# Joining two key classes of a softmax by copies and a one-input reduce in place of small two-input operations

## The chip, the cores and the metric

The kernel runs on one core of a Trainium2 chip. The metric is device time in microseconds (us), the median of several executions; lower is better. The engines are TensorE (PE, matrix products; PEld is its loading of weights), VectorE (DVE), ScalarE (ACT), GpSimd (POOL) and SyncE (SP, which issues the DMAs here). Each engine works through its own list of instructions in the order written, and waits at an instruction until what that one needs is there.

## The reference

All data are f32. With x of 4 sequences x 1024 positions x 1024 features, 32 heads of 32 features, it computes

```python
x = x + attention(layernorm(x), wq, wk, wv, wo)      # rotary q and k, causal softmax
x = x + ffn(layernorm(x), route_w, A, Bw)            # each token goes to the best of 8 rank-16 adapters

scores = jnp.einsum('bqhd,bkhd->bhqk', q, k) * scale
scores = jnp.where(causal, scores, finfo.min)
probs  = jax.nn.softmax(scores, axis=-1)
out    = jnp.einsum('bhqk,bkhd->bqhd', probs, v).reshape(b, s, d) @ wo
```

The softmax needs the largest score of each row (query) and the sum of its exponentials. Those are the "maxima" and "totals" of the title.

## The kernel before, in words

**Units.** The attention is done in 32 units (`attend`): 4 sequences x 8 groups of 4 heads. While one unit's softmax runs, PE also has dense work for other units: the projections to q, k and v (`group`, the products `pa_*` and `pb_*` of line 816) and, for finished sequences, the output projection and the adapters (`finish_tile`, `po` of line 1389, `ph`, `pf`).

**A tile of scores.** A unit has 16 tiles t of 64 queries, handled in 11 rounds (`ROUNDS`): the eight long tiles one to a round, the eight short ones in rounds of 2, 2 and 4. The 128 partitions of a tile hold four groups i of 32: two halves of 32 queries, and for each half two *classes of keys*, the even and the odd blocks of 32 keys. So every row of the softmax is split over two neighbouring groups of partitions, i and i ^ 1, and both its maximum and its total have to be joined across them.

**Steps of a round.** PE makes the scores `s` in PSUM (line 1027); there is one such buffer of four banks, and the value products `av` use it too. ACT copies them to SBUF (`pr` or `pr_low`, line 1060). POOL adds the causal mask on the diagonal (line 1066). DVE takes each class's negated maximum (`top`, line 1088) with `tensor_reduce`. DVE joins the classes (`both`, line 934, in `with_other`): four `tensor_tensor` minima, one for each group of 32 partitions, whose two inputs lie in different groups. ACT computes the exponentials with `both` as bias and leaves each class's sum in `den` (line 1121, an ACTIVATE and a READ_ACCUMULATOR for each head). DVE transposes the blocks of 32x32 (line 1145). After the last round of a quad (4 tiles) PE multiplies by the values (`apply_quad`, `av`, line 1190), and ACT takes the result out of PSUM (`at`, line 1230).

**Totals.** After half a unit (a block, 64 in all) `finish_block` joins the two classes of `den` with four DVE additions (`rec_sb`, line 1254), takes reciprocals (1255), transposes them (1257), sends them through DRAM to spread them over partitions (`by`), and POOL multiplies (`at`, line 1285).

**Layer norm.** `moments` (lines 373 to 386) makes mean, variance, the inverse deviation `rstd` and `less`, which is minus mean times `rstd`. `scale_x` (line 437) applies it on DVE for 8 tiles of the first sequence; elsewhere ACT applies `rstd` and `less`.

**What sets the order.** Nothing is issued where it stands in the source. Every step is a `Task` with an engine, a guessed duration, a due position `pos` (lower is sooner) and the tasks and buffers that it needs. `Plan.order` simulates the five engines once, when the kernel is built, and so writes the order of each engine's instructions. The planner gives `both` 0.72 us. Scores are form "S" on PE, values form "V", all else "D". Three constants matter here: `FETCH`, the time that the planner grants for a block of 256 PE instructions to be fetched; `PATIENCE`, a time after its readiness in which a value task is passed over if PE has other work; `SIGNAL`, the delay from one engine to another.

Of the kernel before, what the change touches and what calls it, by code (L numbers as in the profile page):

```python
# [9 lines left out]
F32 = mybir.dt.float32  # L10
AF = mybir.ActivationFunctionType
ALU = mybir.AluOpType
AX = mybir.AxisListType

P = 128
# [4 lines left out]
SQ = 32  # L20
# [8 lines left out]
DENSE = 0.859  # L29


CHANGE, BLOCK, FETCH = 0.2, 256, 4.5

PATIENCE = 1.0


def act_us(n):
    return 0.05 + 0.000836 * n


def dve_us(n):
    return 0.09 + 0.00103 * n
# [33 lines left out]
class Plan:  # L76
# [23 lines left out]
    def order(self):  # L100
# [91 lines left out]
        def finished(t, now):  # L192
            for b in {id(b): b for b in [*t.uses, *t.opens]}.values():
                b.users -= 1
                if not b.users:
                    at(now + (0.5 if b.slots.name[0] != "_" else 0.25), (b,))
            far = SIGNAL.get(t.engine, 0.1)
            for x in t.next:
                near = x.engine == t.engine and x.engine != "SP"
                when = now + (0.0 if near else far)  # L200
                came[x.number] = max(came.get(x.number, 0.0), when)
                x.waits -= 1
                if not x.waits:
                    at(came[x.number], x)
# [54 lines left out]
def tile_preln_attn_then_top1_lora(  # L259
# [104 lines left out]
    def moments(pos, src, name, after):  # L364

        got = {}

        def stats(i):
            if i == 0:
                got["st"] = small.tile(  # L370
                    [P, D // HALF, nc.vector.BN_STATS_DIM], F32, tag="stats", bufs=5, name=f"st_{name}"
                )
            nc.vector.bn_stats(got["st"][:, i, :], src.tile[:, i * HALF : (i + 1) * HALF])

        def gather():
            got["mv"] = small.tile([P, nc.vector.BN_AGGR_DIM], F32, tag="mv", bufs=5, name=f"mv_{name}")
            nc.vector.bn_aggr(got["mv"], got["st"])
            got["ve"] = small.tile([P, 1], F32, tag="ve", bufs=5, name=f"ve_{name}")
            nc.vector.tensor_scalar(got["ve"], got["mv"][:, 1:2], EPS, None, ALU.add)
            got["less"] = got["mv"][:, 1:2]  # L380
            nc.vector.tensor_scalar(got["less"], got["mv"][:, 0:1], -1.0, None, ALU.mult)

        def power():
            got["rstd"] = small.tile([P, 1], F32, tag="rstd", bufs=5, name=f"rstd_{name}")
            nc.gpsimd.tensor_tensor(got["rstd"], got["ve"], half_sb, ALU.pow)
            nc.gpsimd.tensor_tensor(got["less"], got["less"], got["rstd"], ALU.mult)

        t = None
        for i in range(D // HALF):
            t = add("DVE", 0.61, lambda i=i: stats(i), pos, [after[i], t], [src])  # L390
        t = add("DVE", 0.45, gather, pos, [t])
        t = add("POOL", 0.8, power, pos, [t, cleared])
        return got, t
# [29 lines left out]
    def take_x(b, t, pos):  # L423
        src = sbuf(rows if t % 5 > 2 else feeds, [P, D], f"x_{b}_{t}", "x")
        load = add(
            "SP",
            0.4,
            lambda: nc.sync.dma_start(src.tile, x[b, t * P : (t + 1) * P, :]),
            pos,
            opens=[src],  # L430
            size=P * D * 4,
        )
        soon = pos - FIRST
        got, m = moments(soon, src, f"a{b}_{t}", [load, load])

        def scale_x():
            nc.vector.tensor_scalar(
                src.tile, src.tile, got["mv"][:, 0:1], got["rstd"], ALU.subtract, ALU.mult
            )

        m = add("DVE", 0.75, scale_x, soon, [m], [src])
        tb, k = divmod(t, TB)

        both = [A[b, f"A{tb + 1}{half + 1}"] for half in range(2)]

        def keep(half):
            if k == 0:
                return [], [], [both[half]]
            return [turned_x[b, t - 1, half]], [both[half]], []

        def dst(half):
            return both[half].tile[:, :, k * P : (k + 1) * P]

        for half, d in enumerate(turn(dst, src, f"a{b}_{t}", soon, [m], keep)):
            turned_x[b, t, half] = d
# [471 lines left out]
    def width(k):  # L927
        return (QUADS - 1) * pitch(k) + QUADS * (k + 1) * SQ

    def with_other(dst, src, op):  # L930

        for i in range(P // SQ):
            r, o = slice(i * SQ, (i + 1) * SQ), slice((i ^ 1) * SQ, ((i ^ 1) + 1) * SQ)
            nc.vector.tensor_tensor(dst[r], src[r], src[o], op)  # L934

    total_cols = sum((t + 1) for r in ROUNDS[0] for t in r)
    prob_ready, av_done = {}, {}

    def attend(b, g):
        u = b * NG + g  # L940
# [63 lines left out]
        for tiles in rounds:  # L1004
# [74 lines left out]
            for k, t in enumerate(tiles):  # L1079
                step = HG if t < 8 else 2  # L1080
                for h in range(0, HG, step):

                    def top(k=k, t=t, h=h, step=step, got=got, n=n, tiles=tiles):
                        if "top" not in got:
                            got["top"] = small.tile(
                                [P, n, HG], F32, tag=f"top{n}", bufs=3, name=f"top_{u}_{tiles[0]}"
                            )
                        nc.vector.tensor_reduce(  # L1088
                            got["top"][:, k, h : h + step],
                            place(t)[:, h : h + step, :],  # L1090
                            AX.X,
                            ALU.max,
                            negate=True,
                        )

                    reduced.append(
                        add(
                            "DVE",
                            dve_us(step * (t + 1) * SQ),
                            top,  # L1100
                            pos - 20,
                            [masked[t]],
                            [quads[quad]],
                        )
                    )

            def join(got=got, n=n, tiles=tiles):
                got["both"] = small.tile(
                    [P, n, HG], F32, tag=f"both{n}", name=f"both_{u}_{tiles[0]}", bufs=9 if n == 1 else 3
                )  # L1110
                with_other(got["both"], got["top"], ALU.min)

            joined = add("DVE", 0.72, join, pos - 20, reduced)
            for k, t in enumerate(tiles):
                blk = t // 8
                of_t = []
# [55 lines left out]
    def apply_quad(u, quad, pos, where, vt, loads, turned, of_blk):  # L1172
# [33 lines left out]
        for i in range(n):  # L1206
            js = range(i * nj // n, (i + 1) * nj // n)
            last = add(
                "PE",
                0.01 + 0.215 * len(js),  # L1210
                lambda js=js: piece(js),
                pos - 60,
                [*turned, *loads, last],
                [pr, vt, whole],
                [whole] if i == 0 else [],
                form="V",
                ins=32 * len(js),
            )
        blk, second = divmod(quad, 2)
        if blk not in of_blk:  # L1220
            of_blk[blk] = {"done": sbuf(dones, [P, HALF], f"at_{u}_{blk}"), "steps": []}
# [3 lines left out]
        for half in range(2):  # L1225

            def take(half=half):
                dst = done.tile.rearrange("p (q t s k) -> p q s t k", q=2, s=2, k=SQ)
                src = whole.tile[:, half, : QUADS * SQ].rearrange("p (t k) -> p t k", k=SQ)
                nc.scalar.copy(dst[:, second, half], src)  # L1230

            of_blk[blk]["steps"].append(
                add(
                    "ACT",
                    act_us(QUADS * SQ),
                    take,
                    pos - 100,
                    [last],
                    [whole, done],
                    [done] if first_of_block and half == 0 else [],  # L1240
                )
            )

    def finish_block(b, g, blk, pos, exps, dens, of_blk):
        u = b * NG + g
        done, steps = of_blk[blk]["done"], of_blk[blk]["steps"]
        got = {}

        def join_sums():
            of_den = dens[blk].rearrange("p (t c) h -> p c h t", c=2)  # L1250
            rec = rec_sb[:, blk, : HG * TB].rearrange("p (h t) -> p h t", t=TB)
            for i in range(P // SQ):
                r, o = slice(i * SQ, (i + 1) * SQ), slice((i ^ 1) * SQ, ((i ^ 1) + 1) * SQ)
                nc.vector.tensor_tensor(rec[r], of_den[r, i % 2], of_den[o, i % 2], ALU.add)  # L1254
            nc.vector.reciprocal(rec_sb[:, blk, : HG * TB], rec_sb[:, blk, : HG * TB])
            got["turned"] = small.tile([P, SQ], F32, tag="recT", name=f"recT_{u}_{blk}")
            nc.vector.transpose(got["turned"], rec_sb[:, blk])

        t = add("DVE", 1.2, join_sums, pos - 20, [*exps[blk], cleared])
        there = dram.tile(  # L1260
            [HG * TB, P // SQ, SQ], F32, tag=f"recs{u}_{blk}", name=f"recs_{u}_{blk}"
        )
# [392 lines left out]
```

## Time and profile before

| what | us |
|---|---|
| median of 3 runs | 2819.16 (2813.59 to 2820.26) |
| the profiled execution, its own time | 2805.12 |
| its span, from the first to the last instruction | 2802.9 |
| DVE busy in the span | 2216.6 |
| ACT busy in the span | 1862.3 |
| POOL busy in the span | 1007.0 |

The profiled execution is one run beside the three, some 14 us under their median. The profile counts an engine as busy while one of its instructions executes; PE's matmuls are pipelined and their ends are modelled. A row of waits counts the time in which an engine stood idle and names the work that released it. The chain of waits goes back from the last instruction, at every step to what released it or to the instruction before it on the same engine. "issue" is time in which an engine waited for nothing that the profile shows. The mean granted clock of TensorE was 0.976 of full speed.

### The profile page before, as it was taken

The page shows a single profiled execution, that of the slowest core. Times are in us where ns is not written, and L with a number is a line of the kernel's source. Part 1 is how long each engine was busy: PE and PEld are TensorE (multiplying, and loading weights), DVE is VectorE, ACT ScalarE, POOL GpSimd, SP SyncE. Part 2 cuts the span into 40 slices and gives each one's busy share as a digit, 9 for nine tenths or more (in the row PEclk, how much of TensorE's full clock was granted, in tenths as well). Part 3 has the DMA queues.
Part 4 walks back from the last instruction along what each step waited for, and adds up shares of the span by engine and source line. Part 5 has one row for each costly group of instructions (what it writes and reads, how often), then busy time and mean ns, then how long its engine had stood idle before and what let it go on. Part 6 is the DMA issues. An engine that isn't in the chain of part 4 may idle for free.

```text
span 2802.9 us, 100252 instructions
## 1 busy us (share of the span) xinstructions
PE 2606.1 (93%) x41960; PEld 1277.9 (46%) x41960; DVE 2216.6 (79%) x4450; ACT 1862.3 (66%) x5320; POOL 1007.0 (36%) x1227
## 2 busy tenths in 40 slices
PE   7888989899999999999989999999999999989898
PEld 6433444444444444444444444444444444444454
DVE  7786887989788897888898886789788777977632
ACT  2585766778678687777777785667577565865511
POOL 3437464534353423333333442323333232331100
PEclk9989999999999999999999999999999999999999
DMA  5545354854457757655666675665756555565221
GB/s 176 156 132 178 111 170 127 251 154 124 139 166 210 223 168 258 203 169 169 198 191 191 207 222 156 199 237 175 210 152 194 164 159 177 172 210 174 92 88 55
DMA packets 398500, 484.01 MB, mean 173 GB/s; under 512 B 37856, under 2 KB 252128, under 8 KB 395360
## 3 DMA queue, kind: packets, MB, share of 16 engines
q1 hardware_dynamic: 398048, 477.62, 56.0%
q8 instruction: 329, 5.39, 0.8%
q14 instruction: 123, 1.01, 0.1%
HBM read 358.47 MB, written 119.01 MB: 170 GB/s over the span
## 4 chain that ended last, share of the span: by engine, by line
PE 54%; DVE 29%; ACT 5%; issue 4%; POOL 3%; DMA 2%; SPq 0%; POOLq 0%; ACTq 0%; DVEq 0%
PE po L1389 12%; DVE top L1088 9%; PE pa_qk L816 8%; PE av L1190 8%; PE s L1027 7%; DVE both L934 7%; PE pb_qk L816 6%; DVE pr L1145 6%; PE pa_v L816 4%; PE pb_v L816 3%; ACT pr_low L1121 2%; PE ph L1448 2%; PE pf L1523 2%; DVE rec_sb L1254 1%; DVE pr_low L1145 1%
## 5 line engine op out<-in xcount | busy, mean ns | idle before, releaser
L1121 ACT ACTIVATE pr<-pr,both 128x512 f32<-128x512 f32 (+7 forms) x1024 | 635.7, 634 | 71.6 <-DVE both L934 70.6
L1088 DVE TENSOR_REDUCE top<-pr 128x2 f32<-128x768 f32 (+7 forms) x512 | 477.5, 970 | 126.3 <-POOL pr L1066 124.9
L1389 PE MATMUL po<-wo,attn 128*128 128x512 f32 x1024 | 502.5, 615 | 2.2 <-DMA wo<-in_wo 1.5
L1145 DVE STREAM_TRANSPOSE pr<-pr 128x768 f32<-128x768 f32 (+7 forms) x512 | 481.7, 983 | 11.7 <-ACT pr L1121 8.5
L1121 ACT ACTIVATE pr_low<-pr_low,both 128x256 f32<-128x256 f32 (+7 forms) x1024 | 412.6, 416 | 68.6 <-DVE both L934 68.3
L1060 ACT COPY pr<-s 128x2048 f32<-128x2048 f32 (+7 forms) x256 | 381.0, 1488 | 95.5 <-PE s L1027 84.4
L1027 PE MATMUL s<-k,q 32*32 32x256 f32 (+7 forms) x16384 | 389.5, 407 | 50.4 <-ACT pr L1060 23.9
L934 DVE TENSOR_TENSOR both<-top 32x4 f32<-32x4 f32 (+2 forms) x1408 | 370.0, 263 | 29.2
L1066 POOL TENSOR_TENSOR pr<-pr,causal_sb 128x128 f32<-128x128 f32 x256 | 116.8, 456 | 635.7 <-ACT pr L1060 623.7
L1190 PE MATMUL av<-pr,val 64*32 64x128 f32 (+2 forms) x14336 | 241.3, 270 | 82.5 <-issue 50.6
L1027 PEld LDWEIGHTS s<-k,q 32*32 32x32 f32 x16384 | 155.8, 104 | 327.2 <-ACT pr L1060 107.2
L1190 PEld LDWEIGHTS av<-pr,val 64*32 64x32 f32 x14336 | 206.4, 108 | 186.5 <-issue 127.2
L1389 PEld LDWEIGHTS po<-wo,attn 128*128 128x128 f32 x1024 | 183.1, 193 | 209.5 <-issue 194.9
L1230 ACT COPY at<-av 128x128 f32<-128x128 f32 x256 | 54.9, 267 | 272.5 <-PE av L1190 272.5
L729 POOL TENSOR_TENSOR r_qk<-r_qk,cos_sb 128x512 f32<-128x512 f32 x124 | 158.2, 1276 | 215.8 <-DVE swq L720 98.5
L816 PE MATMUL pa_qk<-A,T_qk 128*128 128x512 f32 x440 | 214.4, 607 | 0.0
L1088 DVE TENSOR_REDUCE top<-pr_low 128x4 f32<-128x1024 f32 (+7 forms) x256 | 177.7, 739 | 41.5 <-POOL pr_low L1066 40.9
L1121 ACT ACTIVATION_READ_ACCUMULATOR pr<-pr,both 128x1 f32 x1024 | 209.0, 204 | 0.0
L1145 DVE STREAM_TRANSPOSE pr_low<-pr_low 128x1024 f32<-128x1024 f32 (+7 forms) x256 | 184.3, 753 | 29.6 <-ACT pr_low L1121 27.7
L1121 ACT ACTIVATION_READ_ACCUMULATOR pr_low<-pr_low,both 128x1 f32 x1024 | 205.8, 201 | 0.0
L1060 ACT COPY pr_low<-s 128x1024 f32<-128x1024 f32 (+7 forms) x256 | 147.7, 639 | 80.9 <-PE s L1027 80.8
L1066 POOL TENSOR_TENSOR pr_low<-pr_low,causal_sb 128x128 f32<-128x128 f32 x256 | 112.0, 455 | 231.6 <-ACT pr_low L1060 228.3
(128 smaller groups left out, 3680.7 us busy)
## 6 DMA issues: line engine op xcount, KB each, us to landing
wo<-in_wo SPq DMA_DIRECT2D x352, 256.0 KB, 3.5
val<-vd SPq DMA_DIRECT2D x128, 256.0 KB, 5.6
T_qk<-t_qk SPq DMA_DIRECT2D x96, 256.0 KB, 3.5
x<-in_x SPq DMA_DIRECT2D x32, 512.0 KB, 5.4
q<-qd SPq DMA_DIRECT2D x128, 128.0 KB, 3.6
b_qk<-in_wq SPq DMA_DIRECT2D x64, 256.0 KB, 3.8
k<-kd SPq DMA_DIRECT2D x32, 512.0 KB, 5.2
vd<-vt SPq DMA_DIRECT2D x64, 256.0 KB, 3.2
```

The lines of the kernel that those rows point to most:

```text
L729: lambda: nc.gpsimd.tensor_tensor(raw.tile, raw.tile, cos_sb[:, cols], ALU.mult),
L816: nc.tensor.matmul(at.tile, lhsT=buf.tile[:, c, :], rhs=act.tile[:, c, :], start=first_ and c == 0, stop=c == KC - 1, skip_group_check=not ...
L934: nc.vector.tensor_tensor(dst[r], src[r], src[o], op)
L1027: nc.tensor.matmul(s.tile[i * SQ : (i + 1) * SQ, h, at : at + w].rearrange("p (j k) -> p j k", k=SQ), lhsT=of_q[r, 2 * (t % QUADS) + half] ...
L1060: nc.scalar.copy(place(t), s.tile[:, :, at : at + w])
L1066: nc.gpsimd.tensor_tensor(diagonal, diagonal, causal_sb.unsqueeze(1).to_broadcast([P, HG, SQ]), ALU.add,)
L1088: nc.vector.tensor_reduce(got["top"][:, k, h : h + step], place(t)[:, h : h + step, :], AX.X, ALU.max, negate=True,)
L1121: nc.scalar.activation(pr[:, h, :], pr[:, h, :], AF.Exp, bias=got["both"][:, k, h : h + 1], accum_out=den(blk)[:, t % 8, h : h + 1],)
L1145: nc.vector.transpose(pr, pr)
L1190: nc.tensor.matmul(whole.tile[h * HD : (h + 1) * HD, half, t0 * SQ : QUADS * SQ].rearrange("p (t k) -> p t k", k=SQ), lhsT=vt.tile[r, h, j ...
L1389: nc.tensor.matmul(po.tile, lhsT=at.tile[:, c * P : (c + 1) * P], rhs=w.tile[:, c % KC] if kept else w.tile, start=c == 0, stop=c == NC - 1,)
L1448: nc.tensor.matmul(ph.tile, lhsT=yn.tile[:, c * P : (c + 1) * P], rhs=w.tile[:, c if kept else c - c0, :], start=c == 0, stop=c == NC - 1,)
```

## The change

The maxima are joined in two steps: `top` gets a second column for each head, four ACT copies write the other class's maxima into it (`swap_classes`, a task of its own ahead of the exponentials), and one DVE `tensor_reduce` over the two columns gives the minimum. The totals are treated alike: four ACT copies of `den` into `denx`, four additions, which now run on POOL, and the reciprocal and transpose on DVE as a task of its own. In the planner FETCH goes from 4.5 to 4.8, PATIENCE from 1.0 to 0, and LATE is new: a task of form S or V that waits for another engine's work counts as ready 1.0 us later. Two dependencies are added (a quad's values wait for the values before them in the unit; the copies out of PSUM wait for the block's first). In the layer norm two results overwrite their inputs, and `scale_x` multiplies by `rstd` and adds `less`.

```diff
-CHANGE, BLOCK, FETCH = 0.2, 256, 4.5
-
-PATIENCE = 1.0
+CHANGE, BLOCK, FETCH = 0.2, 256, 4.8
+
+PATIENCE = 0.0
+
+LATE = 1.0
...
-                when = now + (0.0 if near else far)
+                when = now + (0.0 if near else far + LATE * (x.form in "SV"))
...
-            got["ve"] = small.tile([P, 1], F32, tag="ve", bufs=5, name=f"ve_{name}")
-            nc.vector.tensor_scalar(got["ve"], got["mv"][:, 1:2], EPS, None, ALU.add)
-            got["less"] = got["mv"][:, 1:2]
-            nc.vector.tensor_scalar(got["less"], got["mv"][:, 0:1], -1.0, None, ALU.mult)
+            got["ve"], got["less"] = got["mv"][:, 1:2], got["mv"][:, 0:1]
+            nc.vector.tensor_scalar(got["ve"], got["ve"], EPS, None, ALU.add)
+            nc.vector.tensor_scalar(got["less"], got["less"], -1.0, None, ALU.mult)
...
-                src.tile, src.tile, got["mv"][:, 0:1], got["rstd"], ALU.subtract, ALU.mult
+                src.tile, src.tile, got["rstd"], got["less"], ALU.mult, ALU.add
...
-    def with_other(dst, src, op):
+    def swap_classes(dst, src):
         for i in range(P // SQ):
             r, o = slice(i * SQ, (i + 1) * SQ), slice((i ^ 1) * SQ, ((i ^ 1) + 1) * SQ)
-            nc.vector.tensor_tensor(dst[r], src[r], src[o], op)
+            nc.scalar.copy(dst[r], src[o])
...
-                                [P, n, HG], F32, tag=f"top{n}", bufs=3, name=f"top_{u}_{tiles[0]}"
+                                [P, n, HG, 2], F32, tag=f"top{n}", bufs=3, name=f"top_{u}_{tiles[0]}"
...
-                            got["top"][:, k, h : h + step],
+                            got["top"][:, k, h : h + step, 0],
...
+            def swap(got=got):
+                swap_classes(got["top"][:, :, :, 1], got["top"][:, :, :, 0])
+
...
-                with_other(got["both"], got["top"], ALU.min)
-
-            joined = add("DVE", 0.72, join, pos - 20, reduced)
+                nc.vector.tensor_reduce(got["both"], got["top"], AX.X, ALU.min)
+
+            swapped = add("ACT", 4 * act_us(n * HG), swap, pos - 100, reduced)
+            joined = add("DVE", dve_us(2 * n * HG), join, pos - 50, [swapped])
...
-                [*turned, *loads, last],
+                [*turned, *loads, last or values_done.get(u)],
...
-                    [last],
+                    [last, *of_blk[blk]["steps"][:1]],
...
+        def swap():
+            got["den"] = small.tile([P, 2 * QUADS, HG], F32, tag="denx", name=f"denx_{u}_{blk}", bufs=1)
+            swap_classes(got["den"], dens[blk])
+
         def join_sums():
-            of_den = dens[blk].rearrange("p (t c) h -> p c h t", c=2)
             rec = rec_sb[:, blk, : HG * TB].rearrange("p (h t) -> p h t", t=TB)
             for i in range(P // SQ):
-                r, o = slice(i * SQ, (i + 1) * SQ), slice((i ^ 1) * SQ, ((i ^ 1) + 1) * SQ)
-                nc.vector.tensor_tensor(rec[r], of_den[r, i % 2], of_den[o, i % 2], ALU.add)
+                r = slice(i * SQ, (i + 1) * SQ)
+                pair = [d[r].rearrange("p (t c) h -> p c h t", c=2)[:, i % 2] for d in (dens[blk], got["den"])]
+                nc.gpsimd.tensor_tensor(rec[r], *pair, ALU.add)
+
+        def turn_sums():
             nc.vector.reciprocal(rec_sb[:, blk, : HG * TB], rec_sb[:, blk, : HG * TB])
...
-        t = add("DVE", 1.2, join_sums, pos - 20, [*exps[blk], cleared])
+        t = add("ACT", 4 * act_us(2 * QUADS * HG), swap, pos - 20, [*exps[blk]])
+        t = add("POOL", 0.8, join_sums, pos - 20, [t, cleared])
+        t = add("DVE", 0.45, turn_sums, pos - 20, [t])
```

More of the change, by code (lines that the diff above doesn't have):

```diff
@@ L928, in width @@
         return (QUADS - 1) * pitch(k) + QUADS * (k + 1) * SQ
-    def with_other(dst, src, op):
+    def swap_classes(dst, src):
         for i in range(P // SQ):
             r, o = slice(i * SQ, (i + 1) * SQ), slice((i ^ 1) * SQ, ((i ^ 1) + 1) * SQ)
-            nc.vector.tensor_tensor(dst[r], src[r], src[o], op)
+            nc.scalar.copy(dst[r], src[o])
     total_cols = sum((t + 1) for r in ROUNDS[0] for t in r)
-    prob_ready, av_done = {}, {}
+    values_done = {}
     def attend(b, g):
@@ L1218, in apply_quad @@
             )
+        values_done[u] = last
         blk, second = divmod(quad, 2)
```

## The prediction

> **What bounds the kernel now.** I read the page's busy shares first, then its chain of waits, then the list of who waited for whom for TensorE (PE) alone, then groups by shape, then the timeline of a few microseconds in the middle.
>
> Page, first part and fourth part:
>
> ```profile
> PE 2606.1 (93%) x41960; PEld 1277.9 (46%) x41960; DVE 2216.6 (79%) x4450; ACT 1862.3 (66%) x5320; POOL 1007.0 (36%) x1227
> ...
> PE 54%; DVE 29%; ACT 5%; issue 4%; POOL 3%; DMA 2%; SPq 0%; POOLq 0%; ACTq 0%; DVEq 0%
> PE po L1389 12%; DVE top L1088 9%; PE pa_qk L816 8%; PE av L1190 8%; PE s L1027 7%; DVE both L934 7%; PE pb_qk L816 6%; DVE pr L1145 6%; PE pa_v L816 4%; PE pb_v L816 3%; ACT pr_low L1121 2%; PE ph L1448 2%; PE pf L1523 2%; DVE rec_sb L1254 1%; DVE pr_low L1145 1%
> ```
>
> PE is busy 93% of a span of 2802.9 us, so at most about 197 us can go without making PE's own work shorter. Yet the chain runs through VectorE (DVE) for 29%, and through `both`, 1408 instructions on at most 32x16 elements, for 7%, 196 us. So PE is the bound that is never far, and DVE decides when the next attention matmul may start. What PE really stands still for is in its waits (total us, times, longest):
>
> ```profile
> PE av L1190 <- issue: 54.9, 36, 4.4
> PE s L1027 <- ACT pr L1060: 23.9, 18, 3.3
> PE av L1190 <- DVE pr L1145: 17.1, 14, 3.4
> PE s L1027 <- ACT pr_low L1060: 15.8, 10, 3.9
> PE av L1190 <- DVE pr_low L1145: 14.1, 6, 5.4
> ...
> PE s L1027 <- ACT at L1230: 9.3, 7, 2.0
> ...
> PE av L1190 <- ACT pr_low L1121: 7.8, 1, 7.8
> ```
>
> Scores (`s`) wait for ScalarE (ACT) to empty the one PSUM buffer: 23.9 + 15.8 + 9.3 = 49.0 us. Values (`av`) wait for transposes and exponentials: 17.1 + 14.1 + 7.8, and 8.4 in three smaller rows, 47.4 us. Together 96.4 us is what faster maxima can win on PE. Another 54.9 us is "issue": PE waits for nothing that the profile shows. The other 46 us belong to transposes, weights and the end, which the change hardly touches.
>
> Why `both` costs what it does, from the timeline (start, duration, engine, line) and groups (busy us, mean ns, idle before):
>
> ```profile
> 1404.04 1.28 POOL L737 TENSOR_TENSOR swk<-swk,sin_sb 128x512 f32<-128x512 f32 x1
> 1404.33 2.84 DVE L934 TENSOR_TENSOR both<-top 32x8 f32<-32x8 f32 x4
> 1405.69 1.27 POOL L745 TENSOR_TENSOR r_qk<-r_qk,swk 128x512 f32<-128x512 f32 x1
> 1408.04 1.37 ACT L1060 COPY pr_low<-s 128x512 f32<-128x512 f32 x4
> ```
>
> ```profile
> L934 DVE TENSOR_TENSOR both<-top 32x4 f32<-32x4 f32 x1024 | 254.2, 248 | 21.2
> L1121 ACT ACTIVATION_READ_ACCUMULATOR pr<-pr,both 128x1 f32 x1024 | 209.0, 204 | 0.0
> L1060 ACT COPY pr_low<-s 128x512 f32<-128x512 f32 x32 | 18.2, 569 | 7.7 <-PE s L1027 7.7
> L1060 ACT COPY pr_low<-s 128x128 f32<-128x128 f32 x32 | 8.9, 277 | 0.0
> L1475 DVE TENSOR_REDUCE best<-rank 128x1 f32<-128x8 f32 x32 | 5.2, 161 | 1.1
> L386 POOL TENSOR_TENSOR mv_a<-mv_a,rstd_a 128x1 f32<-128x1 f32 x32 | 6.1, 189 | 2.5
> ```
>
> Four tiny minima at 1404.33 take 2.84 us; one of them starts under the POOL instruction that runs from 1404.04 and ends with it, another likewise with that of 1405.69. Counted over the trace: 1016 of the 1408 overlap no POOL instruction and take 156 ns on average; 392 do and take 540 ns. `tensor_reduce` (`top`) shows no such thing: 887 ns without, 900 ns with POOL beside it. A round's four with the gaps between them take 0.707 us at the median, 1.10 us at the mean, over 352 rounds 387 us.
>
> **The change part by part.**
>
> *Maxima.* Removed from DVE: 352 rounds x 1.10 = 387 us. Added to DVE: 352 reduces of 8 to 32 elements, no wait on POOL, by the `best` row 0.161 us: 57 us. Added to ACT: 352 x 4 copies of 4 to 16 elements. None is in the trace. The nearest rows are score copies: (569 - 277) / 384 = 0.76 ns an element, so 4 elements take 277 - 124 x 0.76 = 183 ns; and four copies that would take 569 + 477 + 376 + 277 = 1699 ns (the group's four shapes) stand in 1.37 us, so each hides 0.11 us behind the next. Four tiny ones: 4 x 0.183 - 3 x 0.11 = 0.40 us; 352 x 0.40 = 141 us of ACT. Lower end 0.30 us (the shortest distance from the start of a 512-element copy to the next instruction's is 465 ns, of a 128-element one 145 ns, so 0.83 ns an element and 38 ns each besides, plus one full duration): 106 us. Upper end no overlap at the READ_ACCUMULATOR's 204 ns: 0.82 us, 287 us. I take 0.40.
>
> The Trainium skill ("ScalarE: Activation LUTs", What ACT_TABLE_LOAD costs) speaks against such copies: it gives a small instruction 186 ns and back-to-back ones an overlap of only about 93 ns. By that page, an estimate, a round is 0.48 us and ACT gets 169 us.
>
> *Latency of one round.* From the last `top` to the exponential it was 0.707 (1.10 on average) and then a hop of 0.09 us (the minima that began at 1400.44 ended at 1401.97, the exponential they released began at 1402.06). It becomes a hop of 0.09, copies 0.40, a hop back of 0.03 (the trace's median from exponential to waiting transpose), 0.16, and the last hop as before: 0.68 us. With POOL quiet nothing is won; on the average 0.42 us a round. On the chain that is 196 x 0.42 / 1.10 = 75 us, if PE didn't stop it earlier.
>
> *The new wait.* The copies stand in ACT's queue and wait for `top`. Behind them stand copies of scores, on which PE waits now for 49.0 us, and exponentials. ACT already stood for `both` 70.6 + 68.3 = 138.9 us in 82 waits, and would now split that wait in two. It has 940 us idle in all, which hides 141 us where the order gives it room.
>
> *Totals.* 64 blocks. Off DVE: 74.4 us of L1254. Onto ACT four copies of 32 elements: 0.40 + 4 x 28 x 0.00076 = 0.49 us, 31 us in all (25 to 58 by the bounds above). Onto POOL four additions of 16 elements, between L386's 189 ns and the 455 ns of the 128-element mask: 0.2 us each, 51 us (48 to 116), in an engine with 1796 us idle. Ahead of them in POOL's queue are masks; behind them the division, which waits for DMAs anyway. Their latency is hidden by the two DMA passages of the reciprocals. Cost on the path: 0; without that cover 64 x 0.8 = 51 us.
>
> *Normalisation.* Same instructions in number; `scale_x` takes a product formed on POOL that it had waited for already. Eight instructions, 7 us: 0. The two ordering dependencies (values after the unit's earlier values, `take` after the block's first) follow PSUM's one buffer, or lie on ACT itself: 0.
>
> So DVE: 2217 - 387 - 74 + 57 = 1813 us (65%); ACT: 1862 + 141 + 31 = 2034 us (73%).
>
> *Order.* The written order comes from the planner. LATE lets a value, once transposed, be placed a full microsecond later; PATIENCE did this only while other work was at hand. Scores depend on PE and loads, so LATE reaches few of them. The order moves, and with it SP's loads and POOL's divisions; nothing in the trace prices that, so -20 to +40 us: an `av` start can at best lose its 31.2 us for DVE (of which I count some elsewhere), at worst leave the score copies as late again as now (49.0 less what the copies win). I take 0. FETCH tells the planner that 256 instructions take 4.8 instead of 4.5 us to come. It can win between 0 and the 54.9 us of "issue"; I take 5.
>
> The skill ("Runtime: NRT & Kernel Launch", Instruction fetch mechanics) has crossings of a 256-instruction block mostly hidden. By that page FETCH is worth 0 and the sum 5 us less; the 36 waits of 1.5 us on `av` are at least some that something doesn't hide.
>
> *Sum on PE.* Of the 47.4 us of values I let two thirds go, since DVE has 404 us less to do and it is DVE's rows that they name: -32. Of the 49.0 us of scores one third, since ACT waits less but carries 172 us more: -16. FETCH -5. Total -53 us: 2805.1 - 53 = 2752 for an execution like the profiled one. That one was 14 us under the median shown, 2819.2, and the difference goes over: 2766 us. What is late next: ACT's score copies and masks on POOL.
>
> **Rivals.**
>
> 1. *All waits go* (0.18). DVE and ACT keep ahead all the time: -96 and part of the issue, -20: 2703 us. For it: the chain's 75 us for `both` and 29% DVE. Against it: ACT is fuller.
> 2. *The freed time reaches nobody* (0.08). PE's order is fixed and 93% full; DVE idles more and the waits move from DVE to ACT: 2819, within 8 us. For it: the 75 us lie beside a busy PE.
> 3. *ACT becomes the gate* (0.17), the slower side. Place: the four copies in ACT's queue ahead of a score copy. At 0.82 us a round and 0.9 a block ACT gets 287 + 58 = 345 us, stands at 2207 us (79%, as full as DVE was), and each late `top` now stops the score copy behind. If half of today's 96.4 us is added, +48: 2867 us. It decides from the point where the copies cost ACT more than the 0.42 us that a round wins, so just above my 0.40; that is why it isn't small.
>
> **How the numbers follow.** Forecast 2766 with 0.57, its own spread 2730 to 2805. With the rivals 0.18, 0.08 and 0.17. The range reaches down to 2700, where half of rival 1 lies below, and up to 2855, where two thirds of rival 3 lie above: some 2 in 10 are out. A difference under 0.3% (8 us) can't be told from none here. Faster 0.75, same 0.08, slower 0.17.
>
> **What would show it.** Right: L934 a reduce at about 160 ns with no tail; copies of 183 ns in chains of about 0.4 us; DVE near 1810 us, ACT near 2030; PE's waits for `DVE pr` and `DVE pr_low` at a third of 31 us; `both` almost gone from the chain. Wrong: a large new wait of ACT for `DVE top` with score rows on PE above 49 us (rival 3), or PE's waits unchanged in sum (rival 2). A change of "issue" by tens of microseconds would mean that the order, not the maxima, moved the time.

## The result, and the profile after

The changed kernel takes 2893.59 us (median of 4 runs, 2891.06 to 2894.93); the kernel before takes 2816.38 us on the same chip. The ratio is 1.0272, with a 95% interval of 1.0254 to 1.0290: 77 us slower. The prediction had 2766 us.

The page of the changed kernel, busy time by engine, and the rows of the new instructions (busy us, mean ns, idle before):

```profile
PE 2614.8 (91%) x41960; PEld 1274.6 (44%) x41960; DVE 1827.9 (63%) x3138; ACT 2223.6 (77%) x6984; POOL 1067.1 (37%) x1483
...
L935 ACT COPY top<-top 32x4 f32<-32x4 f32 (+2 forms) x1408 | 273.1, 194 | 42.5 <-DVE top L1089 23.5
...
L1115 DVE TENSOR_REDUCE both<-top 128x4 f32<-128x8 f32 (+2 forms) x352 | 57.1, 162 | 245.1 <-ACT top L935 242.1
```

VectorE did what was expected: from 2216.6 to 1827.9 us (1813 was worked out), the new reduce at 162 ns. ScalarE went from 1862.3 to 2223.6 us, 361 us more, where 172 were worked out. What PE stands still for (total us, times, longest):

```profile
PE s L1028 <- ACT pr L1061: 62.2, 74, 3.1
PE av L1195 <- issue: 39.5, 23, 4.0
PE s L1028 <- ACT at L1236: 29.6, 26, 3.3
PE s L1028 <- ACT pr_low L1061: 26.0, 27, 3.0
PE av L1195 <- ACT pr L1061: 19.5, 22, 2.5
...
PE av L1195 <- ACT at L1236: 10.3, 7, 3.0
...
PE av L1195 <- ACT pr_low L1061: 9.7, 8, 2.5
...
PE av L1195 <- DVE pr_low L1150: 5.2, 6, 1.2
```

The waits of values for DVE's transposes fell from 31.2 us to 5.6 (a row of 0.4 us isn't shown). The waits of scores for ACT rose from 49.0 to 62.2 + 29.6 + 26.0 = 117.8 us. And the values, rid of DVE, now wait for ACT: 19.5 + 10.3 + 9.7 = 39.5 us, where it was 16.2. Summed over all of PE's waits by the engine that ends them, DVE fell from 50.6 to 19.1 us and ACT rose from 77.0 to 191.9; all of PE's waits together rose from 192 to 270 us, about the 77 us of the result. So the load moved from one engine to another, and the wait with it, and grew on the way. (The chain of waits of this profile breaks off: its shares add up to about 20% of the span, so nothing is read from it.)

Why a round's copies cost ACT so much is in its timeline (start, duration, engine, line):

```profile
2001.15 0.19 ACT L1126 ACTIVATION_READ_ACCUMULATOR pr<-pr,both 128x1 f32 x1
2001.24 1.63 ACT L1061 COPY pr<-s 128x1792 f32<-128x1792 f32 x1
2002.90 0.80 ACT L935 COPY top<-top 32x4 f32<-32x4 f32 x4
2003.73 0.59 ACT L786 COPY r_qk<-pa_qk 128x512 f32<-128x512 f32 x1
```

Four copies take 0.80 us: 193 ns each and 205 ns from one start to the next. Nothing overlaps; the first even begins 0.03 us after the score copy ends, where the score copy itself, on 128 partitions, began 0.1 us before the end of the instruction ahead (2001.24 against 2001.34).

### The profile page after: what moved, and what is told of

Its sections match the earlier page's. It is cut to its first block, busy times and chain, and to the rows that moved or that the text cites. A ratio compares the mean times of both kernels' runs of the same rounds, so it can differ in the third digit from the quotient of the medians.

```text
span 2889.3 us, 101115 instructions
## 1 busy us (share of the span) xinstructions
PE 2614.8 (91%) x41960; PEld 1274.6 (44%) x41960; DVE 1827.9 (63%) x3138; ACT 2223.6 (77%) x6984; POOL 1067.1 (37%) x1483
## 5 line engine op out<-in xcount | busy, mean ns | idle before, releaser
L1150 DVE STREAM_TRANSPOSE pr<-pr 128x768 f32<-128x768 f32 (+7 forms) x512 | 498.5, 993 | 89.4 <-ACT pr L1126 87.9
L1028 PE MATMUL s<-k,q 32*32 32x224 f32 (+7 forms) x16384 | 393.9, 408 | 123.3 <-ACT pr L1061 62.2
L935 ACT COPY top<-top 32x4 f32<-32x4 f32 (+2 forms) x1408 | 273.1, 194 | 42.5 <-DVE top L1089 23.5
L1195 PE MATMUL av<-pr,val 64*32 64x128 f32 (+2 forms) x14336 | 226.6, 264 | 54.4 <-issue 36.5
L1150 DVE STREAM_TRANSPOSE pr_low<-pr_low 128x1024 f32<-128x1024 f32 (+7 forms) x256 | 196.7, 772 | 110.9 <-ACT pr_low L1126 109.5
L1195 PEld LDWEIGHTS av<-pr,val 64*32 64x32 f32 x14336 | 197.2, 106 | 154.7 <-issue 99.5
L1115 DVE TENSOR_REDUCE both<-top 128x4 f32<-128x8 f32 (+2 forms) x352 | 57.1, 162 | 245.1 <-ACT top L935 242.1
L1126 ACT ACTIVATION_READ_ACCUMULATOR pr_low<-pr_low,both 128x1 f32 x1024 | 193.6, 189 | 0.0
L1126 ACT ACTIVATION_READ_ACCUMULATOR pr<-pr,both 128x1 f32 x1024 | 193.6, 189 | 0.0
```

Of the source, the lines that this page charges most:

```text
L935: nc.scalar.copy(dst[r], src[o])
L1028: nc.tensor.matmul(s.tile[i * SQ : (i + 1) * SQ, h, at : at + w].rearrange("p (j k) -> p j k", k=SQ), lhsT=of_q[r, 2 * (t % QUADS) + half] ...
L1115: nc.vector.tensor_reduce(got["both"], got["top"], AX.X, ALU.min)
L1126: nc.scalar.activation(pr[:, h, :], pr[:, h, :], AF.Exp, bias=got["both"][:, k, h : h + 1], accum_out=den(blk)[:, t % 8, h : h + 1],)
L1150: nc.vector.transpose(pr, pr)
L1195: nc.tensor.matmul(whole.tile[h * HD : (h + 1) * HD, half, t0 * SQ : QUADS * SQ].rearrange("p (t k) -> p t k", k=SQ), lhsT=vt.tile[r, h, j ...
```

## The experiments

Each kernel is compared with the kernel before on the same chip; ratios have their 95% intervals. The kernel before took 2808 to 2817 us on the chips used, so times of different rows compare to about 9 us only, and the ratios compare more closely.

| kernel | us | ratio to before |
|---|---|---|
| constants_only | 2830 | 1.0062 (1.0039 to 1.0085) |
| maxima_only | 2883 | 1.0254 (1.0216 to 1.0293) |
| totals_only | 2798 | 0.9942 (0.9923 to 0.9962) |
| joins_only | 2919 | 1.0372 (1.0344 to 1.0400) |
| one_copy | 2700 | 0.9622 (0.9595 to 0.9648) |
| eight_copies | 3199 | 1.1399 (1.1373 to 1.1424) |
| no_shift4 | 2865 | one run, no interval |
| same_place | 2832 | 1.0063 (1.0046 to 1.0081) |
| told_costs | 2765 | 0.9851 (0.9833 to 0.9868) |
| half_told | 2803 | 0.9947 (0.9929 to 0.9965) |
| over_told | 2915 | 1.0341 (1.0309 to 1.0373) |
| told_maxima | 2815 | 0.9985 (0.9965 to 1.0005) |
| told_oldconst | 2732 | 0.9719 (0.9697 to 0.9742) |
| before_told | 2815 | 1.0011 (0.9993 to 1.0030) |
| before_undertold | 2908 | 1.0340 (1.0317 to 1.0363) |
| dve_swap | 2716 | 0.9666 (0.9642 to 0.9689) |
| dve_swap_oldconst | 2685 | 0.9528 (0.9506 to 0.9550) |

My first theory, A, was that ACT's added work is the loss. Its rival, B, was the written order: first that the new constants spoiled it, later that the planner was told wrong durations for the new tasks.

### Which part of the change

constants_only is the kernel before with the three constants; maxima_only and totals_only have one join each; joins_only is the change without the constants.

> The kernel before with the three planner constants of the change alone (FETCH 4.8, PATIENCE 0, LATE 1.0). Theory A, ACT is the gate (a copy costs ACT 205 ns from start to start, 395 us in all, and that is what PE waits for): the constants are worth little, 2800 to 2822 us beside 2816 before. Theory B, the written order is the cause (values and scores placed too late): most of the 77 us is here already, 2870 to 2895 us.

> The kernel before with the maxima joined by ACT copies and one reduce (and the layer norm's reuse of columns, which frees the bytes for it); totals, constants and dependencies as before. Theory A: 352 rounds x 0.93 us are five sixths of the added ACT time, so five sixths of the 77 us, about 2880 us (2860 to 2895); PE's waits for ACT in the score rows rise from 49 to some 100 us. Theory B: no loss, 2765 to 2825 us.

> The kernel before with the totals joined by ACT copies and POOL additions (and the layer norm's reuse of columns) alone. Theory A: 64 x 1.07 us of ACT, a sixth of the loss, about 2830 us (2816 to 2840). Theory B: as before, 2808 to 2824 us.

> The changed kernel with the planner's constants of before (FETCH 4.5, PATIENCE 1.0, no LATE): both joins, without the new constants. Theory A: 2880 to 2905 us, as the changed kernel's 2894. Theory B: the loss is gone, 2770 to 2825 us.

The constants alone cost 0.6%, a little outside what A allowed, but not the 77 us. The maxima alone cost 2.5%, nearly all, as A had it and B in its first form had not. The totals alone *win* 0.6%, against A: 59 us more on ACT (1921.1 busy) and yet faster. With both joins the constants win 25 us (2919 to 2894). So the maxima carry the loss, but "ACT's load" cannot be the whole story.

### The dose of copies, in one and the same order

The planner is told the same in these four, and the order of all other instructions is the same on every engine as in the changed kernel; only the round's four copies differ. one_copy, no_shift4 and same_place leave out the swap, so they are probes and no versions of the kernel. The two replacements below belong to two kernels.

```diff
-                swap_classes(got["top"][:, :, :, 1], got["top"][:, :, :, 0])
+                nc.scalar.copy(got["top"][:, :, :, 1], got["top"][:, :, :, 0])          # one_copy
+                for i in range(4):                                                       # no_shift4
+                    nc.scalar.copy(got["top"][i * SQ : (i + 1) * SQ, :, :, 1], got["top"][i * SQ : (i + 1) * SQ, :, :, 0])
```

eight_copies calls `swap_classes` twice; same_place makes three copies of the first 32 partitions and one of all 128.

> The changed kernel with the four swapping copies of a round replaced by one copy of all 128 partitions that swaps nothing (so the two classes keep different maxima; the planner is told the same, and the written order is the same but for the three copies fewer). Theory A (ACT's time for the copies is the loss): 352 x 3 x 0.205 = 216 us less on ACT; at the 0.2 us of time for a us of ACT seen so far some 45 us less, 2835 to 2860 us. Theory B (the planner placed things wrongly because it was told 0.05 us a copy, or the detour through ACT costs its two crossings): little changes, 2875 to 2895 us.

> The changed kernel with each round's four swapping copies made twice over (same order and planner costs otherwise). Theory A: 352 x 4 x 0.205 = 289 us more on ACT, 2950 us or above, more than 0.2 of the added time, since ACT is fuller. Theory B: 2890 to 2915 us.

> The changed kernel with four copies a round of 32 partitions that stay in their own partitions (no swap, so the classes keep different maxima). If the shift between partitions is what keeps one copy from overlapping the next, the distance from start to start falls from 205 ns towards 100 ns or less and the time to about 2850 us; if it is the small size, or copies whose source lies in SBUF, it stays at 205 ns and 2894 us.

> The changed kernel with a round's four copies made as three of the first 32 partitions into themselves and one of all 128 (nothing is swapped, so the classes keep different maxima; the written order is that of the changed kernel). In the run no_shift4 only the copies that begin at another partition than the one before lost their overlap. If that is the cause, these four stand about 95 ns apart instead of 205, a round costs ACT some 0.4 us, as the prediction took it, and the time falls by about 352 x 0.45 = 160 us to 2715 to 2770 us. If it is the 32 partitions, they stay 205 ns apart and the time at 2850 to 2895 us.

ACT's busy time and the time, from the four profiles and runs: 1955 and 2700 us, 2149 and 2832, 2224 and 2894 (the change itself), 2494 and 3199; the single run of no_shift4, 2188 and 2865, lies between. Between the first and the change 194 us of time for 268 of ACT (0.72; 0.69 by the ratios), from there to eight copies 305 for 271 (1.13; 1.17 by the ratios). The last is above 1 because busy time leaves out the gaps between copies: with them the eight hold ACT 0.9 us longer a round than the four, some 320 us in all. Both theories had expected less than that: A had 0.2 of the added time or somewhat more, B almost nothing. In an order that stays as it is, seven tenths of what comes on top on ACT goes through to the end, and beyond the change's dose all of it, on an engine that is idle for a quarter of the span.

one_copy, ACT's copies and the reduce behind them (by shape: busy us, mean ns, idle before), and PE:

```profile
PE 2583.1 (96%) x41960; PEld 1269.0 (47%) x41960; DVE 1804.9 (67%) x3138; ACT 1955.4 (72%) x5928; POOL 1064.9 (39%) x1483
```

```profile
L1109 ACT COPY top<-top 128x4 f32<-128x4 f32 x256 | 51.9, 203 | 8.7 <-DVE top L1089 8.2
L1115 DVE TENSOR_REDUCE both<-top 128x4 f32<-128x8 f32 x256 | 36.1, 141 | 34.8 <-ACT top L1109 34.1
```

One copy of 128 partitions lasts 203 ns, but the next instruction starts 95 ns after its start: 0.1 us a round, *less* than the 0.21 us that the planner had been told. There PE is at 96%, and the probe is faster than the kernel before.

What stops the overlap is not settled. The shift isn't it alone: in no_shift4 the first copy, of the first 32 partitions, overlapped the instruction ahead by 0.1 us again, but the other three stood 203 ns apart, though none of them waits for another. same_place was to test the beginning partition: its three copies of the same 32 partitions stood 225 ns apart, and only the copy of all 128 let the next one start after 100 ns. But it does not decide. Its copies all write the same place, and by its trace each one behind the first waits on a semaphore that ACT alone raises, that is, for the end of the copy ahead; the copies of the change and of no_shift4 have no such wait. So what is left fits one condition, untested by a run of its own: an instruction that begins at another group of 32 partitions than the one ahead, in what it reads or writes, does not overlap it. The change's copies do so all four, and the instruction behind them too; in no_shift4 the first copy doesn't, and it alone overlaps. The time of same_place, 2832, lies under its expectation for "32 partitions" by 18 us; its first copy overlapped the instruction ahead and its last the one behind.

### What the planner was told

The changed kernel tells its planner `4 * act_us(n * HG)`, 0.21 us, for a round's copies, `4 * act_us(2 * QUADS * HG)`, 0.31 us, for a block's. By ACT's busy time in maxima_only and totals_only they take (2162 - 1862) / 352 = 0.85 and (1921 - 1862) / 64 = 0.92 us.

```diff
-            swapped = add("ACT", 4 * act_us(n * HG), swap, pos - 100, reduced)
-            joined = add("DVE", dve_us(2 * n * HG), join, pos - 50, [swapped])
+            swapped = add("ACT", 4 * (0.2 + 0.0012 * n * HG) + 0.1, swap, pos - 100, reduced)
+            joined = add("DVE", 0.16, join, pos - 50, [swapped])
...
-        t = add("ACT", 4 * act_us(2 * QUADS * HG), swap, pos - 20, [*exps[blk]])
+        t = add("ACT", 4 * (0.2 + 0.0012 * 2 * QUADS * HG) + 0.1, swap, pos - 20, [*exps[blk]])
```

That is told_costs; it tells 0.92 us for a round of one tile and 1.05 us for a block, about a tenth above these means. half_told and over_told put 0.5 and 1.8 in the first line; told_maxima leaves the last line as it was; told_oldconst is told_costs with the constants of before.

> The changed kernel with the planner told what was measured: 0.9 us for a round's copies, 1.05 us for a block's, 0.16 us for the reduce (0.2, 0.3 and 0.1 before). Theory A: ACT's load is the same, the order only gives way around it, 2870 to 2900 us. Theory B (an order made on wrong durations): most of the loss goes, 2800 to 2845 us.

> The changed kernel with the planner told 0.5 us for a round's copies (0.21 in the change, 0.9 measured), the rest as in told_costs. If the loss is the time that the planner doesn't know of, it lies between 2894 and 2765 us, about 2825 (0.43 us a round, 151 us, unknown). If told_costs won only because its order happened to be a good one, no such step is to be expected.

> The changed kernel with the planner told 1.8 us for a round's copies, twice what they take. If only being told too little hurts, it is within 30 us of told_costs' 2765 (ACT believed to be 90% busy makes the order somewhat worse); if truth is a sharp optimum, or the order a matter of chance, it is 2830 us or above.

> The changed kernel told the truth of the maxima (0.9 us for the copies, 0.16 for the reduce), with the totals' copies at 0.30 us as in the change (1.05 measured). The maxima's unknown time is 252 us, the totals' 48 us: five sixths of the 128 us between 2894 and 2765 return, 2770 to 2800 us.

> The changed kernel told the measured durations, but with FETCH 4.5, PATIENCE 1.0 and no LATE. With new constants it was 2765 us. If the constants help as they did with the joins told wrongly (2919 to 2894), 2775 to 2795; if they cost as they did on the kernel before (0.6%), 2745 to 2765.

told_costs does the very same work and is 128 us faster than the change (118 by the ratios). Its page and the rows of PE that answer to those above:

```profile
PE 2590.1 (94%) x41960; PEld 1276.5 (46%) x41960; DVE 1830.1 (66%) x3138; ACT 2225.3 (81%) x6984; POOL 1067.3 (39%) x1483
...
PE 56%; ACT 31%; issue 5%; DVE 3%; DMA 3%; POOL 2%; SPq 1%; POOLq 0%; ACTq 0%; DVEq 0%
```

```profile
PE s L1028 <- ACT pr L1061: 17.6, 18, 2.3
PE av L1195 <- ACT pr_low L1061: 10.9, 9, 2.5
PE s L1028 <- ACT at L1236: 10.7, 9, 4.3
...
PE s L1028 <- ACT pr_low L1061: 4.5, 6, 1.3
```

ACT is as busy as in the changed kernel (2225.3 against 2223.6 us), but the scores wait 32.8 us for it in place of 117.8, and all of PE's waits for ACT are 60.1 us in place of 191.9. That rules theory A out as it stood: the same load costs the time only in the order made on the wrong durations. ACT is now the second engine of the chain (31%), where DVE was before.

The dose goes the same way up to the truth: with the totals told truly, a round told as 0.5 us gives 2803 us (2825 was expected) and as 0.9 us 2765, and PE's waits for ACT go with it: 191.9 us in the change, 115.4 in half_told, 60.1 in told_costs. told_maxima gives back 79 of the 128 us between 2894 and 2765 (81 of 118 by the ratios), not five sixths; the rest goes with the totals' 48 unknown microseconds, or with the order's chance. But over_told, where I expected 2765 with some 30 us more, took 2915: told too much is as bad as told too little. Where it loses is in its slices (each a fortieth of the span, in tenths):

```profile
PE   7889989999999999999999779999999888854698
...
PEclk9989999999999999999999889999999999966699
```

PE falls to 5 and 4 tenths near the end, with a granted clock of 6 tenths there: it looks as if the order left too little dense work for the last units. Its scores wait 100.2 us for ACT, where told_costs has 32.8. In the changed kernel both rows hold at 9 and 8 up to the last slices.

told_oldconst is faster than both its expectations, 2732 us: with true durations, the constants of before are 33 us better (37 by the ratios). The new constants win (2919 to 2894) only with the joins told wrongly.

### The same falsehood on the kernel before

before_told tells the planner 1.10 us for the four minima and 1.65 us for the totals, before_undertold 0.21 us for the minima; nothing else of the kernel before is touched.

```diff
-            joined = add("DVE", 0.72, join, pos - 20, reduced)
+            joined = add("DVE", 0.21, join, pos - 20, reduced)
```

> The kernel before with nothing changed but what the planner is told: 1.10 us for the four minima (0.72 before) and 1.65 us for a block's totals (1.2), as measured. Theory A (only ACT's load counts): 2805 to 2825 us. Theory B in its present form (what the planner wasn't told of goes through to the end): the minima's 134 us and the totals' 29 us that it didn't know of are planned around, 2750 to 2800 us; then part of what the change seems to win with true durations isn't the change's.

> The kernel before with the planner told 0.21 us for the four minima (0.72 before; they take 1.10), the same falsehood as the change has for its copies, on DVE. Theory B: 180 us more that it doesn't know of, on an engine 79% busy: 2850 us or more. Theory A: 2805 to 2830 us.

Told too little, the kernel before loses 3.4%, more than the change. What stands still is ACT, waiting for DVE:

```profile
ACT pr_low L1121 <- DVE both L934: 128.0, 51, 7.9
ACT pr L1121 <- DVE both L934: 117.6, 85, 4.6
```

245.6 us in place of 138.9, without one instruction more; PE's values wait 58.2 us for DVE in place of 31.2, its scores 69.1 for ACT in place of 49.0. So the falsehood needs neither ACT's copies nor the new constants. Told the mean it won nothing (a miss of theory B). A reason that no run tests: the minima take 0.707 us at the median, which 0.72 already was, and the rest is a tail of collisions with POOL that no single number describes.

### Swapping on DVE

dve_swap makes the swaps by a `tensor_reduce` over one element on DVE, one input each, told 0.17 and 0.19 us. dve_swap_oldconst has the constants of before too.

```diff
-            nc.scalar.copy(dst[r], src[o])
+            nc.vector.tensor_reduce(dst[r], src[o], AX.X, ALU.max)
...
-            swapped = add("ACT", 4 * act_us(n * HG), swap, pos - 100, reduced)
-            joined = add("DVE", dve_us(2 * n * HG), join, pos - 50, [swapped])
+            swapped = add("DVE", 4 * 0.17, swap, pos - 20, reduced)
+            joined = add("DVE", 0.17, join, pos - 20, [swapped])
```

> The changed kernel with the swaps made on DVE by tensor_reduce over one element (one input, so nothing of POOL's holds it), told 0.17 us each for the maxima and 0.19 for the totals; ACT gets no copies. A round costs DVE 5 x 0.17 = 0.85 us instead of 1.10, ACT nothing. Theory A (ACT is the gate) and theory B (true durations) both give less than the 2765 us of told_costs: 2700 to 2755 us.

> The swaps on DVE by one-input reduces as in dve_swap (2716 us), with the planner constants of before. If these constants gain here what they gained with told durations (2765 to 2732), 2680 to 2700 us, faster than every kernel so far that computes the whole; if that gain was a chance of the order, 2705 to 2730 us.

Both came in as expected; dve_swap_oldconst is the fastest kernel of the study, 4.7% under before. Its page, and the swaps by shape:

```profile
PE 2578.0 (96%) x41960; PEld 1264.3 (47%) x41960; DVE 2064.9 (77%) x4802; ACT 1863.2 (69%) x5320; POOL 1064.5 (40%) x1483
...
PE 82%; ACT 5%; DVE 5%; issue 3%; POOL 2%; DMA 2%; SPq 0%; POOLq 0%; ACTq 0%; DVEq 0%
```

```profile
L933 DVE TENSOR_REDUCE top<-top 32x4 f32<-32x4 f32 x1024 | 152.7, 149 | 19.0
L1113 DVE TENSOR_REDUCE both<-top 128x4 f32<-128x8 f32 x256 | 40.9, 160 | 8.1
```

DVE does five small instructions for four, and they take 270 us in all where the minima took 370, since none of them waits for POOL: 149 ns each where the minima took 248 at the mean. With the totals' additions gone to POOL, DVE is 152 us less busy than before. The chain is PE's for 82%, where it was 54%.

## Why the prediction was wrong

**Right: the reading of before.** `both` was slow because of POOL, the reduce costs 0.162 us (0.161 was worked out) and never more than 0.188, DVE came out within 15 us of the sum, POOL gained 60 us (51). (The 15 us are mostly a slip of the sum: the 387 us of the minima had the gaps between them in it, and without these they were busy for 370.) The waits of values for DVE nearly vanished, by more than the two thirds that I let go. That a join without the collision is worth about as much as PE's waits fits dve_swap_oldconst, near the end of rival 1, though its order is another one.

**Wrong: two terms of the sum on PE.** "Of the 47.4 us of values I let two thirds go": 45 us stayed, because ACT took DVE's place in them. "Of the 49.0 us of scores one third": they grew by 69 us. "Issue" on `av`, put at -5, fell by 15. Behind the two terms stand two steps.

**Wrong: the cost of the copies.** The step was "Four tiny ones: 4 x 0.183 - 3 x 0.11 = 0.40 us". The duration was right (0.193), the overlap absent. A round costs ACT 0.85 us, just above the upper end of my bounds. The overlap was taken from copies of 128 partitions that begin at the same one, and these cover 32 and begin at different ones. The Trainium skill ("ScalarE: Activation LUTs", What ACT_TABLE_LOAD costs) gives an overlap of about 93 ns for ACTIVATEs back to back; one_copy is near it (203 ns long, 95 to the next start, 108 of overlap), the copies of 32 partitions aren't (12 ns between end and start).

**Wrong, and what turned the sign: the order, of which I wrote "I take 0".** I weighed LATE, PATIENCE and FETCH, and passed over the durations that the new tasks bring with them: 0.21 us told for what I myself put at 0.40 and bounded at 0.82. My own upper bound stood four times above the number in the diff. I had written that ACT's idle time "hides 141 us where the order gives it room"; this order gave it too little. With the durations true the same instructions, constants and all, take 2765 us: the likeliest time of the prediction (2777 by its ratio, from the 2819 that I set out from), though its term for the copies was wrong by half and so its agreement is partly luck. FETCH was priced at -5 us. "Issue" on `av` did fall, from 54.9 to 39.5 us, but the three constants together are worth +0.6%, -0.9% or +1.2% as the rest of the order has it.

**Rival 3** named the right engine and rows (scores waiting for ACT), its 2207 us of ACT came close (2224), and its 2867 us was the nearest number. The sign that it named beside them did not come: ACT waits only 23.5 us for `top`, so it was not late maxima that stopped the score copies. Its deciding point was wrong: "where the copies cost ACT more than the 0.42 us that a round wins". In told_costs they cost twice that, and the kernel is faster than before.

**What stays open.** Every told duration gives one order, and one order has its chance: that half_told, told_costs and over_told form a valley is three points. That a true duration is better than a fourth of it or less is shown on ACT and on DVE, and on ACT in several orders: told 0.21 us, maxima_only, joins_only and the change lie at 1.025 to 1.037 of before, told 0.92, told_maxima, told_costs and told_oldconst at 0.972 to 0.9985. That 0.9 us is the best number is not shown. What keeps small copies from overlapping isn't settled either.

## What to carry to other kernels

Where instructions are issued in an order computed beforehand, a new task's told duration is part of the change: compare it with the nearest measured rows before anything else, because here work that the order didn't know of went through to the end at 0.7 to 1.2 us for each us, on an engine with a quarter of its time free. Before work is moved to another engine, look whether it is slow by itself or by a collision: here the same engine with one-input instructions beat the other engine. Overlap between neighbouring instructions is to be taken from rows that cover the same partitions in the same sequence. And a probe must not bring in a wait of its own: copies made to write one place, as in same_place, wait for each other whatever else is tested.

## What the runs showed of the hardware

- ACT copies that went through the four groups of 32 partitions one by one did not overlap: 193 ns long and 205 ns apart with the swap, 190 and 203 without it, while a copy of 128 partitions and 4 elements let the next start after 95 ns. The first copy of a round overlapped the instruction ahead by 0.1 us without the swap (no_shift4) and stood 0.02 us behind it with the swap.
- DVE's small `tensor_tensor` with two SBUF inputs took 156 ns without POOL beside it and 540 ns at the mean with it; a `tensor_reduce` of 32x4 took 149 ns at the mean with POOL 40% busy.
